# Two-layer graph attention with top-p sparsification: trial sums of the extra tiles on ScalarE, residuals of the output rows by an identity product

## The chip, the cores and the metric

The kernel runs on one core of a Trainium2 chip. The metric is device time in microseconds (us) of one execution; a lower figure is better. Engines are named as the profile names them: PE (TensorE), DVE (VectorE), ACT (ScalarE), POOL (GpSimd) and SP (SyncE, which here only issues transfers). Each runs its own instructions in order and waits for others by semaphores.

## The reference

There are N = 3327 nodes with D = 256 features, in float32. Layer 0 is a graph attention over a sparse adjacency matrix, followed by a gated recurrent unit, a residual and a layer normalisation. Layer 1 takes its result X (called x1 below) and makes two steps over all nodes:

```
R  = (S + I) / row sums                  # S: the sparse adjacency
for n in 0, 1:
    A  = top_p_attention(Xa)             # softmax of q k^T, then the largest entries of
                                         # each row until their sum reaches 0.9
    Xf = R @ Xf ;  Xa = A @ Xa
    Z  = Z + Xf @ U1[n].T + Xa @ U2[n].T
h   = X + Z
out = layernorm(x1 + (layernorm(h) * ln_g + ln_b))
```

A row's nucleus is found without a full sort: a kept entry is one above a threshold of that row, and the sum of the entries above a trial value tells on which side of the threshold the trial lies.

## The kernel before, in words

Rows are worked on in 26 tiles of 128 (the last has 127). A "product" i is one tile of one step, 0 to 25 in step 0 and 26 to 51 in step 1.

Layer 0 comes first (`Layer0.run`). Towards its end, `first_logits` (L1010) computes the logits of the first two tiles of step 0, group by group as the keys come in, on a list of column chunks (`FIRST_CHUNKS`).

Layer 1 (`Layer1`, from L1120) loads U1, U2, ln_g and ln_b at its start. Then `run` (L1752) loops over the products. Product i multiplies the kept probabilities of tile i with the features (`turn` and `times`: PE transposes, ACT copies `at`, PE products `pav`, in seven groups). Between the groups there are seven slots, and `slot(g, f)` puts other work behind group g: the logits of tile i + 2, the exponentials and the list of the largest entries of tile i + 1, the residue of tile i - 1 (`rest`). `propagate` (L1355) is the sparse product with R: POOL gathers the neighbours' rows (L607) and makes one-hot weights `m` (L1353), PE multiplies (`pxf`, L1361), ACT scales, POOL adds the own row (L1366, L1367), SP stores the result to DRAM.

Rows whose nucleus the fast method does not settle are flagged (`flag`, counted by a small product `pos`, L1486), put aside in a list in DRAM (`left_over`, L1516), and computed again as three "extra" tiles h0, h1 and h2 (`HARD` = 3) with a more thorough method. For an extra tile k:

- `hard_load` (L1521) reads the list from DRAM and gathers the rows (four gathers, one of them later in `hard_gather`).
- `hard_q`, `hard_exp` (L1543, L1562) compute its logits (PE) and their exponentials (ACT), 3327 wide.
- `bound` (L1575) narrows the threshold from above: for each of six factors f in `CUTS` (1/16, 1/4, 1/2, 0.71, 0.84, 0.92) it sums the entries below f times the present bound by one wide DVE pass (`kept_sum`, L1336) and multiplies the bound by f where the sum is large enough. Each trial depends on the one before.
- `hard` (L1592) is the search itself on DVE: one wide pass (L1598), the largest entries of each group of columns, their sort, a scan, three wide replacements (L1330) and a last wide pass (L1627).
- `hard_end` (L1633) is its product with the features and its output rows, `hard_store` (L1659) the scatter of the rows to the output.

`ends` (L1697) follows product 51. It runs the searches of h0, h1 and h2 and, between their steps, the output of the 26 tiles. A tile's output (`tile_end`, L1454) is a generator of some eight stages: loads of xf, xf2 and xa2; transposes and their copies (`ptxut`, `ptxvt`, L1176, L1178); the products with U1 and U2 into `pzt` (L1430); and `output_rows` (L1435). That copies the sum to SBUF (L1438), adds x1 on POOL (L1439), takes mean and variance on DVE (`moments`: L1374, L1376, and two POOL operations at L1377, L1378), normalises on ACT (`normalized`: a shift of 128x1 by POOL at L1384, then L1385), multiplies by ln_g, adds ln_b and adds x1 on POOL (L1445, L1446, L1447), and normalises once more. `tick` opens one tile and moves every open one a stage on. `more` moves the first job of a queue (the start of h2, the ends of h0 and h1) one step, and calls `tick` in every call when the queue was empty and in every second call otherwise. `ends` calls `more` after each step of a trial or a search. Last comes `hard_end` of h2 with its output rows.

In Layer 1 the order on PE, ACT and DVE is that of the program text. The order on POOL and SP is made by a scheduler when the kernel is built.

Of the kernel before, what the change touches and what calls it, by code (L numbers as in the profile page):

```python
# [53 lines left out]
FIRST_CHUNKS = [[(h, s, LC) for h in range(2)] for s in range(0, HALF - LC, LC)] + [  # L54
    [(0, HALF - LC, LC), (1, HALF - LC, LATE - HALF + LC)]
]
# [12 lines left out]

CUTS = tuple(2.0 ** -f for f in (4.0, 2.0, 1.0, 0.5, 0.25, 0.125))  # L70
# [446 lines left out]
class Shared:  # L517


    def __init__(self, tc, ctx, x, W1T, W2T, W3T):  # L520
# [48 lines left out]

        self.xa_rows = dram.tile([N, D], F32, name="xa_rows")  # L570
# [70 lines left out]
class Layer0:  # L641
# [364 lines left out]
    def first_logits(self):  # L1006


        nc, sh = self.nc, self.sh
        while not self.searched:  # L1010
            yield
        for chunks in FIRST_CHUNKS:
            while self.done * P < chunks[-1][0] * HALF + chunks[-1][1] + chunks[-1][2]:
                yield
            for i in range(2):
                on = [slice(h * DA, (h + 1) * DA) for h, _, _ in chunks]
                pls = [
                    self.ps.tile([P, 512], F32, tag="tr", name=f"first{i}_{h}_{s}") for h, s, _ in chunks
                ]
                for pl, half, (h, s, w) in zip(pls, on, chunks):  # L1020
                    nc.tensor.matmul(
                        pl[:, :w], sh.qT[half, cols(i)], sh.kT[half, 0, s : s + w], start=True, stop=True
                    )
                yield
                for pl, (h, s, w) in zip(pls, chunks):
                    nc.scalar.copy(sh.arrays[i][:, h * HALF + s : h * HALF + s + w], pl[:, :w])
                yield
                if i == 0:
                    for h, s, w in chunks:
                        for g in range(s // GROUP[0], (s + w) // GROUP[0]):  # L1030
                            c = h * HALF + g * GROUP[0]
                            at = c // GROUP[0] * 8
                            nc.vector.max(sh.cand[:, at : at + 8], sh.arrays[0][:, c : c + GROUP[0]])
                    yield
# [86 lines left out]
class Layer1:  # L1121
    def __init__(self, sh, ctx, U1T, U2T, ln_g, ln_b, out):
# [12 lines left out]
        nc.scalar.dma_start(self.u1, U1T.rearrange("s (c p) d -> p (s c) d", p=P))  # L1135
        self.u2 = keep.tile([P, STEPS * DC, D], F32, name="u2")
        nc.scalar.dma_start(self.u2, U2T.rearrange("s (c p) d -> p (s c) d", p=P))
        self.g = keep.tile([P, D], F32, name="ln_g")
        nc.scalar.dma_start(self.g, ln_g.partition_broadcast(P))
        self.b = keep.tile([P, D], F32, name="ln_b")  # L1140
        nc.scalar.dma_start(self.b, ln_b.partition_broadcast(P))
# [8 lines left out]
        self.p = [sh.arrays[2][:, :N], keep.tile([P, N], F32, name="p")]  # L1150

# [203 lines left out]
    def propagate(self, i):  # L1355
# [12 lines left out]
        move_rows(nc.sync, (sh.xf2_rows if v.n else sh.xf_rows)[t * P : t * P + r, :], v.xf2, r)  # L1368

# [11 lines left out]
    def normalized(self, dst, src, mv, r, tag):  # L1381
        nc = self.nc
        shift = self.small("shift", f"shift{tag}")
        nc.gpsimd.tensor_scalar(shift[:r], mv[:r, 0:1], mv[:r, 1:2], -1.0, ALU.mult, ALU.mult)  # L1384
        nc.scalar.activation(dst, src, AF.Identity, bias=shift[:r], scale=mv[:r, 1:2])  # L1385
# [49 lines left out]
    def output_rows(self, pz, x1, h, r, tag):  # L1435
# [3 lines left out]
        nc.gpsimd.tensor_tensor(h, h, x1, ALU.add)  # L1439
        yield  # L1440
# [5 lines left out]
        nc.gpsimd.tensor_tensor(h, h, self.b[:r], ALU.add)  # L1446
        nc.gpsimd.tensor_tensor(h, h, x1, ALU.add)  # L1447
# [6 lines left out]
    def tile_end(self, t):  # L1454
# [4 lines left out]
        xa2 = self.work.tile([P, D], F32, tag="xf", name=f"xa2_{t}")  # L1459
        move_rows(nc.sync, a[:r, :D], sh.xf_rows[on, :], r)  # L1460
        move_rows(nc.sync, a[:r, D : 2 * D], sh.xf2_rows[on, :], r)
        move_rows(nc.sync, xa2[:r], sh.xa2_rows[on, :], r)
        yield
# [6 lines left out]
        for n, xt in enumerate(xts):  # L1470
            self.output_terms(pz, xt, n, (0, 1), r, n == 0, n == 1)
        yield

        k = t % (N // D)
        h = sh.qT[:r, k * D : (k + 1) * D]
        yield from self.output_rows(pz, sh.x1[:r, t, :], h, r, f"t{t}")
        move_rows(nc.sync, self.out[on, :], h, r)
# [65 lines left out]
    def hard_q(self, k):  # L1543
# [8 lines left out]
        if k == 1:  # L1552
            a, b = self.p
        else:
            a, b = (self.l[j % 2][:, :N] for j in (k // 2, k // 2 + 1))
        v.p, v.other = a, b

        v.top = self.small("htop", f"top{v.tag}")
# [16 lines left out]
    def bound(self, k):  # L1575
# [3 lines left out]
        v.thr = self.small("hthr", f"thr{tag}")  # L1579
        nc.gpsimd.tensor_scalar(v.thr, v.pay[:, 2:3], 0.5, None, ALU.mult)  # L1580
        for i, f in enumerate(CUTS):
# [5 lines left out]
            nxt = self.small("top", f"top{tag}_{i + 1}")  # L1587
# [45 lines left out]
    def hard_end(self, k):  # L1633
# [20 lines left out]
        self.output_terms(pz, xt, 1, (1,), P, False, True)  # L1654
        v.o = xa
        v.end = self.output_rows(pz, x1, v.o, P, v.tag)
# [40 lines left out]
    def ends(self, bound):  # L1697
# [11 lines left out]
        def more():  # L1709
            self.calls += 1  # L1710
            busy = bool(queue)
            if busy and next(queue[0], True):
                queue.pop(0)
            if not busy or self.calls % 2:
                tick()

        self.calls = 0

        def start(k):
            self.hard_q(k)  # L1720
            for pair in self.chunks():
                yield
                self.hard_exp(k, pair)

# [4 lines left out]
        for _ in start(1):  # L1729
            pass  # L1730
        for _ in bound:
            more()
        for k in range(HARD):
            for j, _ in enumerate(self.hard(k)):
                if k == 0 and j == 2:
# [191 lines left out]
```

## Time and profile before

| | |
|---|---|
| median of the runs | 1890.84 us (1890.25 to 1891.82, 3 runs) |
| the profiled execution | 1894.84 us |
| its span | 1893.1 us |
| mean granted clock of PE | 0.941 |

| stage | from, to (us) | length |
|---|---|---|
| layer 0 | 0 to 432 | 432 |
| step 0 of layer 1 | 432 to about 1010 | 578 |
| step 1 | about 1020 to 1597 | 577 |
| trial sums of h0 | 1597 to 1624 | 27 |
| searches of h0, h1, h2 with the output of the tiles | 1624 to 1847 | 223 |
| product and output of h2 | 1847 to 1893 | 46 |

A span is what the profiler saw from the first to the last instruction; a busy time is the sum of an engine's instructions in a stretch, without issuing of transfers and without waits. In a row of groups the figures behind the bar are busy time, mean duration of one instruction in ns, and the idle time just before them with what ended it. A PE duration is that of one instruction, and several overlap: eight products of 128x256 follow each other in 1.73 us.

### The profile page before, as it was taken

What the parts mean: (1) busy time and instruction counts of PE and PEld (TensorE: products, weight loads), DVE (VectorE), ACT (ScalarE), POOL (GpSimd) and SP (SyncE); (2) the same over time, 40 slices, a digit from 0 to 9 for tenths busy, and PEclk for the clock granted to TensorE, in tenths of its full rate; (3) what the DMA queues carried; (4) which work ended last, traced back from release to release, by engine and by line L of the source; (5) the groups of instructions that cost most, each with busy time, mean ns of one, the idle gap of its engine ahead of it and who ended that gap; (6) DMA issues with size and microseconds to landing.
All of it is one profiled execution on the core that took longest, in us unless ns stands there. A gap on an engine that the chain in (4) does not pass through costs nothing.

```text
span 1893.1 us, 27173 instructions
## 1 busy us (share of the span) xinstructions
PE 1662.6 (88%) x8035; PEld 1218.2 (64%) x8035; DVE 1371.5 (72%) x4318; ACT 918.7 (49%) x2063; POOL 1222.8 (65%) x1900
## 2 busy tenths in 40 slices
PE   6578778987999999999996999999999998988844
PEld 4345545555777777777774777777777676676733
DVE  6789886436556665556654999999999897978771
ACT  3245445544565555565553555555555453434332
POOL 1477778837766666666654566556666574699993
PEclk9789889997999999999997999999999998999977
DMA  9766652212211111111101111111111121212100
GB/s 328 261 213 233 200 172 68 63 35 79 59 40 40 40 42 48 48 40 40 39 29 50 48 49 45 45 48 56 51 48 45 46 59 31 60 59 79 56 28 20
DMA packets 84205, 143.96 MB, mean 76 GB/s; under 512 B 15561, under 2 KB 57283, under 8 KB 84050
## 3 DMA queue, kind: packets, MB, share of 16 engines
q1 hardware_dynamic: 52288, 78.38, 12.4%
q0 software_dynamic: 20384, 53.28, 10.7%
q10 hardware_dynamic: 11378, 10.49, 1.7%
q8 instruction: 66, 1.08, 0.2%
q14 instruction: 89, 0.73, 0.1%
HBM read 117.84 MB, written 24.35 MB: 75 GB/s over the span
## 4 chain that ended last, share of the span: by engine, by line
PE 38%; DVE 33%; POOL 12%; ACT 6%; DMA 6%; issue 4%; ACTq 0%; POOLq 0%; DVEq 0%; SPq 0%
PE pav L1410 18%; DVE array L1330 6%; PE pl L1192 5%; DVE cand L1208 4%; PE pxf L1361 4%; PE pt L1394 4%; DVE cand L1228 3%; DMA g<-whx,edge 3%; POOL g L607 3%; DVE lst L1226 3%; DVE p L1316 2%; DVE array L1316 2%; DVE at L812 2%; ACT at L1396 1%; DMA array<-in_adj_dram 1%
## 5 line engine op out<-in xcount | busy, mean ns | idle before, releaser
L1410 PE MATMUL pav<-xa,at 128*128 128x256 f32 (+2 forms) x1352 | 330.0, 389 | 7.0 <-ACT at L1396 7.0
L1410 PE MATMUL pav<-x,at 128*128 128x256 f32 (+2 forms) x1352 | 326.8, 386 | 7.3 <-ACT at L1396 7.3
L1396 ACT COPY at<-pt 128x512 f32<-128x512 f32 (+2 forms) x364 | 191.9, 541 | 269.3 <-PE pt L1394 268.2
L1410 PEld LDWEIGHTS pav<-xa,at 128*128 128x128 f32 (+2 forms) x1352 | 245.5, 191 | 85.1 <-ACT at L1396 38.9
L1410 PEld LDWEIGHTS pav<-x,at 128*128 128x128 f32 (+2 forms) x1352 | 245.4, 191 | 72.1 <-ACT at L1396 29.7
L1208 DVE MAX8 cand<-array 128x8 f32<-128x167 f32 (+5 forms) x921 | 238.8, 336 | 46.9 <-ACT array L1195 46.9
L1195 ACT COPY array<-pl 128x416 f32<-128x416 f32 (+4 forms) x405 | 182.9, 502 | 183.6 <-PE pl L1192 183.5
L607 POOL DMA_INDIRECT g<-xf_rows,edge x130 | 135.7, 1044 | 164.9 <-PE pxf L1361 132.6
L607 POOL DMA_INDIRECT g<-x_rows,edge x130 | 133.7, 1029 | 128.2 <-PE ptq L620 91.4
L1192 PE MATMUL pl<-kT,qT 64*128 64x416 f32 (+4 forms) x810 | 197.6, 561 | 1.8 <-ACT kT L637 1.8
L1300 DVE TENSOR_TENSOR_SCAN before<-e 128x40 f32<-128x40 f32 (+3 forms) x52 | 14.3, 274 | 216.4 <-ACT e L1293 216.4
L607 POOL DMA_INDIRECT g<-whx,edge x130 | 136.9, 1053 | 46.6 <-issue 31.1
L1353 POOL TENSOR_SCALAR m<-col,erow 128x128 f32<-128x128 f32 x260 | 159.6, 628 | 10.0 <-PE pxf L1361 8.0
L1361 PE MATMUL pxf<-g,m 128*128 128x256 f32 (+1 forms) x520 | 134.5, 408 | 11.2 <-DVE out L1238 5.9
L1361 PEld LDWEIGHTS pxf<-g,m 128*128 128x128 f32 (+1 forms) x520 | 99.4, 200 | 65.7 <-issue 39.6
L1226 DVE MAX8 lst<-cand 128x8 f32<-128x160 f32 (+3 forms) x364 | 114.5, 315 | 9.0
L1394 PE MATMUL pt<-ident,array 128*128 128x128 f32 (+1 forms) x676 | 101.5, 277 | 6.2 <-DVE array L1316 6.2
L812 DVE FIND_INDEX8 at<-ones,array 128x8 uint32<-128x840 f32 (+1 forms) x104 | 106.5, 1026 | 0.0
L1394 PE MATMUL pt<-ident,p 128*128 128x128 f32 (+2 forms) x676 | 100.4, 275 | 4.5 <-DVE p L1316 4.5
L1394 PEld LDWEIGHTS pt<-ident,array 128*128 128x128 f32 (+1 forms) x676 | 85.2, 145 | 24.7 <-PE pxf L1361 8.2
L1394 PEld LDWEIGHTS pt<-ident,p 128*128 128x128 f32 (+2 forms) x676 | 84.6, 144 | 22.0 <-PE pxf L1361 8.6
L965 PE MATMUL prz<-wih,hT 128*128 128x512 f32 (+1 forms) x104 | 68.1, 790 | 34.3 <-ACT hT L963 34.3
(373 smaller groups left out, 3366.0 us busy)
## 6 DMA issues: line engine op xcount, KB each, us to landing
array<-in_adj_dram SPq DMA_DIRECT2D x25, 1248.0 KB
array<-in_adj_dram SPq DMA_DIRECT2D x25, 415.5 KB
xf_rows<-xf SPq DMA_DIRECT2D x50, 128.0 KB
xa_rows<-xa SPq DMA_DIRECT2D x50, 128.0 KB
xfs<-xf_rows SPq DMA_DIRECT2D x50, 128.0 KB
whx<-table ACTq DMA_DIRECT2D x25, 129.5 KB
x_rows<-x ACTq DMA_DIRECT2D x25, 128.0 KB
xf<-xf_rows SPq DMA_DIRECT2D x25, 128.0 KB
```

What stands on the lines that cost most here:

```text
L607: self.nc.gpsimd.indirect_dma_start(out=dst[:, b, :], out_offset=None, in_=table[:, :], in_offset=bass.IndirectOffsetOnAxis(ap=self.edge[: ...
L812: nc.vector.max_index(at[:r, g, :], self.ones8[:r], ad[:r, g, :])
L1192: nc.tensor.matmul(pl[:r, :w], q[on], self.sh.kT[on, n, s : s + w], start=True, stop=True)
L1195: nc.scalar.copy(l[:r, h * HALF + s : h * HALF + s + w], pl[:r, :w])
L1208: self.nc.vector.max(cand[:r, g * 8 : g * 8 + 8], src[:r, g * group : min(N, (g + 1) * group)])
L1226: nc.vector.max(lst[:r, k : k + 8], cand[:r])
L1330: nc.vector.match_replace(rev, gone[:r], rev, -BIG)
L1353: nc.gpsimd.tensor_scalar(v.m[:, b, :], sh.col1, sh.erow[:, v.at, b : b + 1], None, ALU.is_equal)
L1361: nc.tensor.matmul(acc[:r, :D], v.m[:, b, :r], v.g[:, b, :], start=(b == 0), stop=(b == EB - 1))
L1394: nc.tensor.transpose(pt[: rows(j), j - j0, :r], v.p[:r, cols(j)], self.ident[:r, :r])
L1396: nc.scalar.copy(at[:, :full, :r], pt[:, :full, :r])
L1410: nc.tensor.matmul(v.acc[: v.r, :D], at[:k, j - 4 * g, : v.r], V[:k, j, :], start=(j == 0), stop=(j == NT - 1))
```

## The change

1. `FIRST_CHUNKS` is ordered anew: one group of the first half's last columns comes first, and the last group has two chunks of 288 columns in place of two of 416 and two of 288.
2. U1, U2, ln_g and ln_b are loaded by SP's queue instead of ACT's.
3. `propagate` of step 0 also computes xb = x1 + ln_b for each tile (one POOL addition) and stores it in DRAM. `tile_end` loads x1 and xb for its tile, into columns of a buffer that is free by then.
4. In the output rows the first residual is added by a product with the identity matrix into the same accumulation (`plus`), not by POOL. After ln_g, one POOL addition of xb takes the place of two, of ln_b and x1. Extra tiles keep both. The shift is two ACT copies of 128x1 with a scale, no longer a POOL operation.
5. The first trials of an extra tile are computed by ACT (`coarse_bound`): per trial and half of the columns one Relu and one Sign with accumulation, from which nine small POOL operations make the sum and the new bound. h0 has two such trials, in products 50 and 51, and four on DVE; h1 and h2 have three and three.
6. `hard_load` of h0 and h1 moves from slot 5 to slot 0 of product 48; `hard_q` of h0 from product 50 to 48, its exponentials to 49, those of h1 to 50. The probabilities of h0 and h1 lie in what was x1's buffer.
7. In `ends` the start of h2 is queued at once, `tick` runs in every call of `more`, each call also takes up to two steps of the coarse trials, `hard_end` of h2 goes through the queue, and all `hard_store` come last.

```diff
-FIRST_CHUNKS = [[(h, s, LC) for h in range(2)] for s in range(0, HALF - LC, LC)] + [
-    [(0, HALF - LC, LC), (1, HALF - LC, LATE - HALF + LC)]
-]
+FIRST_CHUNKS = [[(i, 0, HALF - LC, LC) for i in range(2)]]
+FIRST_CHUNKS += [[(i, h, s, LC) for h in range(2)] for s in range(0, HALF - LC, LC) for i in range(2)]
+FIRST_CHUNKS += [[(i, 1, HALF - LC, LATE - HALF + LC) for i in range(2)]]
...
-        nc.scalar.dma_start(self.u1, U1T.rearrange("s (c p) d -> p (s c) d", p=P))
+        nc.sync.dma_start(self.u1, U1T.rearrange("s (c p) d -> p (s c) d", p=P))
...
+        if v.n == 0:
+            xb = self.work.tile([P, D], F32, tag="xa2", name=f"xb{t}")
+            nc.gpsimd.tensor_tensor(xb[:r], v.xf, self.b[:r], ALU.add)
+            move_rows(nc.sync, sh.xb_rows[t * P : t * P + r, :], xb[:r], r)
...
-        nc.gpsimd.tensor_scalar(shift[:r], mv[:r, 0:1], mv[:r, 1:2], -1.0, ALU.mult, ALU.mult)
+        nc.scalar.activation(shift[:r], mv[:r, 0:1], AF.Copy, scale=-1.0)
+        nc.scalar.activation(shift[:r], shift[:r], AF.Copy, scale=mv[:r, 1:2])
...
-        nc.gpsimd.tensor_tensor(h, h, x1, ALU.add)
...
-        nc.gpsimd.tensor_tensor(h, h, self.b[:r], ALU.add)
-        nc.gpsimd.tensor_tensor(h, h, x1, ALU.add)
+        for term in terms:
+            nc.gpsimd.tensor_tensor(h, h, term, ALU.add)
...
+        move_rows(nc.sync, x1, sh.x1_rows[on, :], r)
...
+        self.plus(pz, x1, r)
...
+        move_rows(nc.sync, xb, sh.xb_rows[on, :], r)
+        yield from self.output_rows(pz, [xb], h, r, f"t{t}")
...
+    def plus(self, pz, x, r):
+        self.nc.tensor.matmul(pz[:r, :D], self.ident[:r, :r], x, start=False, stop=True)
...
+    def coarse_bound(self, k, cuts, junk):
...
+        for f in cuts:
+            nc.gpsimd.tensor_scalar(minus, v.top, -f, None, ALU.mult)
...
+            for h in range(2):
+                on = slice(h * HALF, min(N, (h + 1) * HALF))
+                for j, func in enumerate((AF.Relu, AF.Sign)):
+                    nc.scalar.activation(
+                        junk[:, on], v.p[:, on], func, bias=minus, accum_out=s[:, 2 * h + j : 2 * h + j + 1]
+                    )
+                    if h == 0 or j == 0:
+                        yield
+            nc.gpsimd.tensor_tensor(both, s[:, 0:2], s[:, 2:4], ALU.add)
+            nc.gpsimd.tensor_scalar(number, both[:, 1:2], 0.5, 0.5 * N, ALU.mult, ALU.add)
+            nc.gpsimd.tensor_tensor(number, number, minus, ALU.mult)
+            nc.gpsimd.tensor_tensor(number, both[:, 0:1], number, ALU.subtract)
+            nc.gpsimd.tensor_scalar(up, number, less, f - 1.0, ALU.is_lt, ALU.mult)
+            nc.gpsimd.tensor_scalar(up, up, 1.0, None, ALU.add)
+            nc.gpsimd.tensor_tensor(nxt, up, v.top, ALU.mult)
...
         def more():
-            self.calls += 1
-            busy = bool(queue)
-            if busy and next(queue[0], True):
+            if queue and next(queue[0], True):
                 queue.pop(0)
-            if not busy or self.calls % 2:
-                tick()
+            tick()
+            for _ in range(2):
+                for g in bounds:
+                    if not next(g, True):
+                        break
...
+        queue.append(start(2))
+        for k in range(HARD):
+            if k:
+                for _ in bounds[k - 1]:
+                    pass
+                for _ in self.bound(k, CUTS[COARSE:]):
+                    more()
+            for _ in self.hard(k):
+                more()
+            queue.append(end(k))
...
-                    slot(5, self.hard_load, 0)
-                    slot(5, self.hard_load, 1)
+                    slot(0, self.hard_load, 0)
+                    slot(0, self.hard_load, 1)
+                if i == total - 4:
+                    slot(6, self.hard_q, 0)
                 if i == total - 2:
-                    slot(3, self.hard_q, 0)
-                    for k, pair in enumerate(self.chunks()):
-                        slot(3 + k, self.hard_exp, 0, pair)
+                    slot(3, self.hard_q, 1)
+                for k, at, first in ((0, total - 3, 0), (1, total - 2, 3)):
+                    if i == at:
+                        for j, pair in enumerate(self.chunks()):
+                            slot(first + j, self.hard_exp, k, pair)
+                if total - 2 <= i:
+                    coarse = self.coarse_bound(0, CUTS[i - total + 2 :][:1], self.l[0][:, :N])
+                    for g in (0, 1, 2, 3) if i == total - 2 else (0, 0, 1, 1):
+                        slot(g, next, coarse, None)
...
                 if i + 1 == total:
-                    bound = self.bound(0)
-                    for g in (1, 3, 5):
-                        slot(g, next, bound)
+                    bound = self.bound(0, CUTS[2:])
+                    bounds = [self.coarse_bound(1, CUTS[:COARSE], self.l[1][:, :N])]
+                    for g in (2, 3, 4, 5, 6):
+                        slot(g, next, bound, None)
+                    for g in (3, 4, 5, 6):
+                        slot(g, next, bounds[0], None)
```

## The prediction

> **What bounds the kernel now.** I read the page first (engines, then the costliest groups), then a table of stretches of the last 300 us, the groups of that stretch, the waits, and single stretches in order of time. On the page:
>
> ```profile
> PE 1662.6 (88%) x8035; PEld 1218.2 (64%) x8035; DVE 1371.5 (72%) x4318; ACT 918.7 (49%) x2063; POOL 1222.8 (65%) x1900
> ```
>
> TensorE leads on average, but the change touches several stages with different limits. Step 0 (432 to 1010 us) runs on TensorE and step 1 (1020 to 1597) on TensorE and VectorE together, at 21.8 us a tile in both. After 1597 comes the end stage. Columns of the next view: stretch, length, busy us (instructions) of PE, weight loads, DVE, ACT, POOL, then clock, DMA share, GB/s.
>
> ```profile
> 1020.00:1590.00 570.00, 532.53 (x2626) 397.87 (x2626) 521.47 (x1628) 292.83 (x572) 340.16 (x588) 0.97 0.17 47
> 1597.00:1624.00 27.00, 24.86 (x113) 17.84 (x114) 25.30 (x29) 11.13 (x24) 21.67 (x9) 0.92 0.21 45
> 1624.00:1847.20 223.20, 171.83 (x851) 143.12 (x851) 182.27 (x385) 79.41 (x167) 192.19 (x291) 0.91 0.18 57
> 1847.20:1893.00 45.80, 22.52 (x105) 18.57 (x103) 3.42 (x14) 9.91 (x20) 14.80 (x30) 0.72 0.06 21
> ```
>
> First the trial sums of extra tile h0, then the three searches on DVE, then h2's product alone. In the 223.2 us no engine is full: POOL 192, DVE 182, PE 172. They wait for each other. The groups after 1597 say how:
>
> ```profile
> L1336 DVE SCALAR_TENSOR_TENSOR array<-array,cndh 128x3327 f32<-128x3327 f32 x12 | 45.2, 3765 | 2.2 <-ACT array L1573 1.7
> L1336 DVE SCALAR_TENSOR_TENSOR p<-array,cndh 128x3327 f32<-128x3327 f32 x6 | 22.9, 3818 | 0.3
> L1374 DVE BATCH_NORM_STATS2 bnbt<-qT 128x6 f32<-128x256 f32 (+1 forms) x26 | 10.9, 421 | 23.6 <-POOL qT L1447 23.5
> L1385 ACT ACTIVATE qT<-qT,shiftbt,mvbt 128x256 f32<-128x256 f32 (+1 forms) x26 | 15.7, 604 | 35.4 <-POOL shiftbt L1384 35.4
> L1384 POOL TENSOR_SCALAR shiftbt<-mvbt 128x1 f32<-128x1 f32 (+1 forms) x26 | 22.5, 865 | 0.7
> L1439 POOL TENSOR_TENSOR qT<-qT,x 128x256 f32<-128x256 f32 (+1 forms) x26 | 18.9, 725 | 6.9 <-ACT qT L1438 6.9
> ```
>
> The 18 trial sums are DVE work; DVE waits 23.5 us for POOL's last residual add, and ACT 35.4 us for POOL's shift, a 128x1 operation of 865 ns. Single instructions tell why it is so long:
>
> ```profile
> 1654.46 3.69 DVE L1627 SCALAR_TENSOR_TENSOR array<-array,th 128x3327 f32<-128x3327 f32 x1
> 1654.55 4.18 POOL L1447 TENSOR_TENSOR qT<-qT,x 128x256 f32<-128x256 f32 x1
> ```
>
> The same add takes 0.73 at 1850: a POOL operation that starts under a wide DVE pass lasts until the pass ends. And in step 1, product 49:
>
> ```profile
> 1569.02 0.16 PE L1486 MATMUL pos<-flag,lower 128*128 128x1 bf16 x1 [8.15 <-POOL flag L1484]
> ```
>
> POOL is late there with the gathers of the extra tiles (1539 to 1551); that product takes 32.5 us instead of 21.8.
>
> **What the Trainium skill says.** "SBUF — State Buffer", Who interferes with whom: a VectorE operation with two SBUF inputs blocks a GpSimd operation that reads SBUF, fully; the 4.18 us above agrees. "ScalarE: Activation LUTs", What ACT_TABLE_LOAD costs: an activation takes about 280 ns + 0.833 ns an element with a pointer operand, 186 + 0.833 with immediates. For 1664 columns that is an estimate of 1.67 us; the trace has 1.684 plus 0.191 for reading the accumulator (L1280). The same section prices a switch of function set at 2.66 us; the built order has no more switches after the change than before, so I add none.
>
> **The change part by part.** Against the profiled execution: 1894.84 us, which is 1893.1 of span and 1.74 outside it; it lies 4.0 us above the median of the runs.
>
> (1) Boundary of the layers. The four weight loads leave ACT's queue (issues from 423.9 to 428.4; the copy after them starts at 428.48) and the last group of first logits has two products of 288 columns instead of four products. The SP queue takes the loads and has room. -3 us (-4 to 0).
>
> (2) xb = x1 + ln_b in step 0: 26 POOL adds of 0.73 (L1439's row) and 26 stores of 128 KB. Two buffers, so an add waits for the store of the one two before; a 128 KB store lands in 1.7 to 1.84 (issue at 457.74, the waiting load at 459.44). Two adds per 2.65 us. In the built order POOL has twenty of them in one block between the own rows of tile 1 (469.3) and the gathers of tile 3, which ran at 490 to 497 and are wanted by TensorE at 509.4. Twenty take 27 us, with one or two caught under a DVE pass 34. The block ends at 497 to 504, the five gathers (6.7) and the m (2.9) at 507 to 514. +3 us (0 to +20), and TensorE at 98.8% in step 0 can't win it back.
>
> (3) Products 48 to 50. hard_load comes five slots earlier: its gathers and the wait for the list leave the place that cost the 8.15, and the clock that dropped behind it (some 2.5). It now stands ahead of the flag in product 48 (+5.5, estimated from two landings of 2.2 and 2.9). hard_q and hard_exp of h0 and h1 move into full products: 16 records at 0.97 for four, 3.9 us of TensorE each, against as much less later; h0's counts here (+3.5), h1's is taken with part 5. Four half-row passes on ACT in product 50 are 7.1, half of it before the list's exponentials: +3.6. Sum +2 (-6 to +8).
>
> (4) h0's trial sums. Before, six passes of 4.36 ran from 1597.9 and the search began at 1624.0. After, two cuts are ACT's. Cut 1/4 needs four passes (1.78 each with overlap) between the at copies of the last product, so about 1600 to 1611, then seven POOL operations (2.2), behind the residual, the index work and six gathers: about 1617. Then four passes, 17.4. Search at 1635 rather than 1624: +11 (+3 to +20). Here the change loses: ACT plus POOL is slower than two DVE passes.
>
> (5) Searches. Of DVE's 182.3 in the long stretch, 6 of 12 passes go: 26.2. The coarse sums of h1 and h2 are 24 ACT passes, 43 us against 144 us of idle ACT. POOL loses L1439 (18.9), both L1384 rows (29.3) and one of L1446/L1447 (25 to 29), and gets some 45 small operations of 0.2 to 0.29. Net some 63 of 192 gone, and fewer long passes to be caught under. Cost: two 128x1 copies instead of each shift, 0.19 and 0.28 by the page's formula (nearest row: 0.297 for L1559), 58 pairs, 27 us of ACT. TensorE: the identity product, 8 records of an equal shape take 1.73, so two take 0.43, 29 of them 13 us. The added loads, 52 of 128 KB at 6 to 9% DMA share, are hidden by the call before.
> DVE needs 156; at 90% it is 173, from 1637 to 1810. TensorE needs 24.9 + 171.8 + 13 - 4 (h1's logits) = 206 from 1599, at the 94% that it held from 1597 to 1700 (96.5 of 103) 219: 1818. They are coupled by the order of the calls, so I take 1820 for the end of h2's search, against 1847.2: -27, of which parts 3 and 4 have already taken 13 back.
>
> (6) The last 45.8. ACT waits 7.0 and 3.7 us for POOL's shifts here, at 1848 and 1853, in front of h2's copies. Both go, as does L1439 in h2's rows (0.73); one identity product and two more row stores come: 39.5 (37 to 44), -6.3.
>
> Sum: -3 + 3 - 27.2 - 6.3 = -33.7; 1861.1 as a profiled run, 1857 on the scale of the median.
>
> **The rivals.**
> A, the ends run better: DVE at 97% in part 5 gives 1798 for h2's search, TensorE following; 1835. For it: POOL was the only engine to hold DVE. Against: TensorE's own 206.
> B, TensorE becomes the bound. tick() at every call puts a tile's 5.7 us beside a quarter of an extra product's 28, 12 us of TensorE in calls where DVE has 5.6. With 85% of TensorE, 206 becomes 242, the search ends at 1841 and the kernel at 1878. For it: 52 us of TensorE idle before; against: much of that was POOL's.
> C, the other side: ACT, in program order, holds TensorE. A trial pass stands between the transposes and the copy that feeds the output product; the 24 passes are 43 us. If all are exposed, 1857 + 43 = 1900. It decides from 34 us on, four passes in five. For it: more() sends up to two steps of trial passes at every call, right behind tick(). Against: DVE needs 5 us a call anyway and ACT 5 to 7.
> D, part 2 costs more: each add waits for its own store behind SP's other transfers, 3.7 us instead of 1.35, block +47 us less 8 of slack: 1857 + 36 = 1893. For it: one POOL queue, twenty in a row; against: the 1.7 us measured.
> That nothing happens: not likely, since six passes and 63 us of POOL leave the stretch that sets the end.
>
> **How the numbers follow.** Forecast (1845 to 1868) 0.50, A 0.12, B 0.20, C 0.11, D 0.07. Runs spread by 0.1% and the profile by 0.2%, so 0.2% (3.8 us) is what a measurement can tell. C ends slower in most of its chance and D in half: slower 0.14, same 0.04, faster 0.82. The range 1834 to 1890 leaves out the fast half of A, and C; with the ends of parts 2 and 4 inside it.
>
> **What would show it.** Ten trial passes (L1336) instead of 18, six of them after h0's; DVE's wait for POOL's last add below 8 us; no shift on POOL. h0's search starts at 1630 to 1640, h2's ends near 1820. In step 0, the product of tile 3 late by 0 to 5 us once. No wait over 4 us on the flag in product 49, a new one in 48. Wrong would be: TensorE idle for ACT's copies for more than 30 us after 1600 (C), POOL's block over 40 us (D), or h0's search later than 1645, with DVE idle for the coarse cut.

## The result and the profile after

The changed kernel takes 1886.91 us (median of 14 runs, 1884.41 to 1889.88), the kernel before 1894.18 us in the 14 runs taken with them. The ratio is 0.9963, with a 95% interval of 0.9953 to 0.9974: about 7 us faster. The forecast was 34 us faster, at 1857. The time lies in the range given, but only a fifth of the gain is there. The profiled execution has a span of 1884.5 us against 1893.1.

The page of the kernel after, busy time by engine:

```profile
PE 1665.2 (88%) x8093; PEld 1223.3 (65%) x8093; DVE 1335.0 (71%) x4278; ACT 997.8 (53%) x2243; POOL 1174.2 (62%) x1881
```

DVE lost 36.5 us and POOL 49, ACT gained 79: the work moved as the change says. The same stretches as in the prediction, with the columns given there: step 1, then from the start of product 51 to h0's search, then the three searches, and last h2's product alone.

```profile
1020.00:1590.00 570.00, 530.21 (x2623) 394.62 (x2623) 519.37 (x1623) 296.81 (x578) 335.81 (x582) 0.97 0.18 49
1608.80:1645.50 36.70, 22.21 (x109) 17.64 (x109) 16.88 (x20) 24.74 (x39) 21.21 (x29) 0.87 0.22 51
1645.50:1844.20 198.70, 173.71 (x889) 147.12 (x888) 151.04 (x348) 129.09 (x297) 126.09 (x216) 0.96 0.30 91
1844.20:1884.50 40.30, 21.35 (x107) 17.82 (x107) 4.73 (x20) 13.61 (x36) 13.82 (x25) 0.80 0.07 24
```

The searches hold 31 us less of DVE's work and 66 less of POOL's, and are 24.5 us shorter. Still no engine is full. The groups of the end stage name the new wait:

```profile
L1337 DVE SCALAR_TENSOR_TENSOR array<-x,cndh 128x3327 f32<-128x3327 f32 x7 | 27.0, 3860 | 0.3
L1337 DVE SCALAR_TENSOR_TENSOR p<-array,cndh 128x3327 f32<-128x3327 f32 x3 | 11.9, 3961 | 0.2
L1379 DVE BATCH_NORM_STATS2 bnbt<-qT 128x6 f32<-128x256 f32 (+1 forms) x26 | 10.9, 419 | 12.2 <-POOL qT L1451 12.1
L1379 DVE BATCH_NORM_STATS2 bnat<-qT 128x6 f32<-128x256 f32 (+1 forms) x26 | 10.6, 406 | 27.1 <-ACT qT L1444 27.1
```

Ten trial passes are left of 18. DVE's wait for POOL's last addition has halved (most of what is left, 8.8, comes after h2's search). In its place DVE waits 27.1 us for the copy of a tile's sum (L1444), which before cost it nothing, and 12.3 us for the same copy of an extra tile's rows. That is 39.4 of the 47.7 us in which DVE stands idle during the searches: it now waits for what TensorE and ACT make.

One edit that the list of the change does not name bears on this. Before, `output_rows` had two `yield`s between a tile's sum and its statistics; now it has one:

```diff
         nc.scalar.copy(h, pz[:r, :D])
-        nc.gpsimd.tensor_tensor(h, h, x1, ALU.add)
-        yield
         yield
         m = self.moments(h, r, f"a{tag}")
```

So DVE asks for a sum one call of `more` earlier than before. No run put the second `yield` back, and how much of the 27.1 us is due to it stays open.

Start by start, this is where the time went. "Later" is measured against the kernel before, in the profiled executions.

| point | before | after | later by | step of the prediction | its forecast | measured |
|---|---|---|---|---|---|---|
| product 1 of step 0 | 465.69 | 463.17 | -2.5 | 1, boundary | -3 | -2.5 |
| product 4 | 531.21 | 533.07 | +1.9 | 2, xb | +3 | +4.4 |
| product 47 | 1494.48 | 1494.83 | +0.4 | change of step, not forecast | 0 | -1.5 |
| product 51 | 1596.85 | 1608.78 | +11.9 | 3, products 48 to 50 | +2 | +11.5 |
| h0's search | 1624.04 | 1645.51 | +21.5 | 4, h0's trials | +11 | +9.5 |
| h2's search ends | 1847.2 | 1844.2 | -3.0 | 5, searches | -40.2 | -24.5 |
| end | 1893.1 | 1884.5 | -8.6 | 6, h2's product | -6.3 | -5.6 |

A product starts with its first `pxf`. (The prediction wrote part 5 as -27.2, with the 13 of parts 3 and 4 in it.) Two steps failed, part 3 by 9.5 us and part 5 by 15.7. The others are within 1.5.

The first three rows are small against the spread of single profiles. Over the sixteen profiled kernels that have xb, product 1 starts at 460.3 to 466.2, product 4 comes 65.7 to 70.1 us after it (65.5 before), and product 47 comes 961.4 to 965.5 us after product 4 (963.3 before). So -2.5, +4.4 and -1.5 are what this one pair shows, not prices.

What is seen in the two places? In product 47, PE in order of time has a wait that the kernel before did not have there, and POOL's queue (some lines left out) says why:

```profile
1523.43 0.16 PE L1497 MATMUL pos<-flag,lower 128*128 128x1 bf16 x1 [6.74 <-POOL flag L1495]
```

```profile
1514.11 0.18 POOL L1539 CAST idxh<-payh 128x1 uint32<-128x1 f32 x1 [2.89 <-DMA payh<-left_over]
1516.41 1.15 POOL L1548 DMA_INDIRECT xh<-xa_rows,idxh  x1 [0.16 <-POOL pay L1511]
1517.64 2.51 POOL L1253 TENSOR_SCALAR many<-d 128x1 f32<-128x1 f32 x1
1520.43 1.11 POOL L1548 DMA_INDIRECT xh<-x_rows,idxh  x1 [0.28 <-issue]
1521.59 0.31 POOL L1254 TENSOR_SCALAR flag<-many,short 128x1 f32<-128x1 f32 x1
```

The load of h0 stands ahead of the flag of the tile. POOL waits for the list to land, gathers, and computes the flag in between. TensorE waits for it.

In product 51, DVE stands until ACT and POOL have done the cut 1/4 of h0 (the form is "who waits for whom: us in all, times, longest"):

```profile
DVE cndh L1625 <- POOL toph_0.25_16379 L1613: 20.0, 1, 20.0
```

In the end stage, ACT in order of time stands for a trial value, TensorE stands for ACT, and POOL, which owes the value, is under DVE's passes:

```profile
1640.77 1.68 ACT L1598 ACTIVATE array<-x,minush_0.25_16522 128x1664 f32<-128x1664 f32 x1 [7.70 <-POOL minush_0.25_16522 L1593]
```

```profile
1644.90 2.25 PE L1578 MATMUL plh<-kT,qh 64*128 64x416 f32 x4 [8.56 <-ACT array L1581]
1692.71 3.78 PE L1416 MATMUL pavh<-xa,ath 128*128 128x256 f32 x8 [9.89 <-ACT ath L1402]
```

```profile
1632.92 3.56 POOL L1610 TENSOR_SCALAR up4h_0.0625_16492<-many4h_0.0625_16488,lessh 128x1 f32<-128x1 f32 x1
1636.56 0.22 POOL L1611 TENSOR_SCALAR up4h_0.0625_16492<-up4h_0.0625_16492 128x1 f32<-128x1 f32 x1
1636.86 0.19 POOL L1613 TENSOR_TENSOR toph_0.0625_16495<-up4h_0.0625_16492,toph 128x1 f32<-128x1 f32 x1
1637.14 3.60 POOL L1593 TENSOR_SCALAR minush_0.25_16522<-toph_0.0625_16495 128x1 f32<-128x1 f32 x1
```

Two of these operations on 128 numbers take 3.6 us, the length of a pass of h0 on DVE; the two between take 0.2. (A trial has eight such operations, and the first trial of a tile one more.) So the trial chain of h1 on ACT and POOL runs into h0's trials on DVE, and what is queued behind it on ACT (h2's exponentials, the tiles' copies, `ath`) waits too. TensorE has 35.5 and 38.3 us busy in the two stretches of 50 us from 1600 to 1700, then 48.0 and 48.9 in the next two. (Before, it had 45.5 and 48.0, then 37.6 and 40.4.)

### The profile page after: what moved, and what is told of

It is laid out like the page before. It is cut to its first block, busy times and chain, and to the rows that moved or that the text cites. A ratio compares the mean times of both kernels' runs of the same rounds, so it can differ in the third digit from the quotient of the medians.

```text
span 1884.5 us, 27520 instructions
## 1 busy us (share of the span) xinstructions
PE 1665.2 (88%) x8093; PEld 1223.3 (65%) x8093; DVE 1335.0 (71%) x4278; ACT 997.8 (53%) x2243; POOL 1174.2 (62%) x1881
## 5 line engine op out<-in xcount | busy, mean ns | idle before, releaser
L609 POOL DMA_INDIRECT g<-x_rows,edge x130 | 140.3, 1079 | 104.4 <-PE ptq L622 71.3
```

The lines of the kernel that those rows point to most:

```text
L609: self.nc.gpsimd.indirect_dma_start(out=dst[:, b, :], out_offset=None, in_=table[:, :], in_offset=bass.IndirectOffsetOnAxis(ap=self.edge[: ...
```

## The experiments

Each changes the kernel after; the lines that matter are shown, and "..." marks what is left out. Ratios are to the kernel before; 0.001 is 1.9 us. The change itself has 0.9963 (0.9953 to 0.9974), and gains and losses against it are differences of ratios. With both intervals, such a difference is good to 3 to 5 us. Readings of a stretch come from one profile of each kernel. Theory T says that ACT, in program order, holds the others at the start of the end stage. B is the prediction's rival that TensorE's own work sets the end. L says that the calls of `more` put too much of TensorE ahead of DVE's next step.

**All six trials of h0 on DVE.**

```diff
-                    coarse = self.coarse_bound(0, CUTS[i - total + 2 :][:1], self.l[0][:, :N])
-                    for g in (0, 1, 2, 3) if i == total - 2 else (0, 0, 1, 1):
-                        slot(g, next, coarse, None)
...
-                    bound = self.bound(0, CUTS[2:])
+                    bound = self.bound(0, CUTS)
```

> The changed kernel with all six trial sums of h0 on DVE and none on ACT; h0's logits and exponentials stay in products 48 and 49. Theory T (ACT, in program order, holds TensorE and DVE at the start of the end stage; TensorE makes up for it later at full load): h0's search starts at 1634 to 1637 in place of 1645.5 (six passes of 4.36 from 1608), ACT has eight passes (14 us) less before 1623, and the end comes 8 to 11 us earlier than with the change: about 1877. Rival B (TensorE's own work from 1611 on sets the end): the search starts as early, but the end moves by 3 us at most.

Measured 1883.22 us, 0.9939 (0.9916 to 0.9962), some 4.5 us better than the change (the two intervals just overlap), half of what T said. Product 51 starts at 1602.9, so that h0's passes on ACT had cost product 50 5.6 of the 11.5 us (it takes 23.7 instead of 29.3). The search starts at 1629, 16.5 us earlier. But it ends at 1673.5 and takes 44.5 us, not 34.6. The waits of this run say why:

```profile
PE plh L1578 <- ACT array L1581: 13.5, 1, 13.5
ACT array L1598 <- POOL minush_0.25_16498 L1593: 12.7, 1, 12.7
```

With more passes on DVE, what stands in POOL's queue, h1's chain and the gathers ahead of it (shown below), is blocked longer, and that takes back what h0 won.

**One step of ACT's trials per call instead of two.**

```diff
-            for _ in range(2):
+            for _ in range(1):
```

> The changed kernel with one step of the trial sums on ACT per call instead of two. Theory T: TensorE's waits for ACT between 1600 and 1700 (9.9 for ath, 8.6 for the exponentials) get shorter and the end comes 3 to 8 us earlier. Rival B: no difference over 2 us. Should the last steps of h1 now stand in a row before its search, DVE shows a wait of 5 us or more there and the end comes later.

1888.18 us, 0.9975 (0.9966 to 0.9984): no gain. DVE's waits for the tiles' sums fall from 27.1 to 11.3 us, but DVE now waits 5.6 and 10.5 us for the last trial ahead of h1 and h2, as the last sentence of the expectation had it. This slower pace moves the wait and does not shorten it.

**No trials on ACT for h1 and h2.**

```diff
-COARSE = 3
+COARSE = 0
```

> The changed kernel with all six trial sums of h1 and of h2 on DVE (h0 keeps its two on ACT). DVE gets six passes of 4.36, 26.2 us, more; ACT loses 24 passes, 43 us. Theory T: what DVE pays comes back from ACT, since TensorE no longer waits 19 us for it before 1700: the end within 5 us of the change's. If DVE set the pace, 18 to 26 us later; if TensorE's own work did, earlier by no more than 3.

1903.46 us, 1.0049 (1.0031 to 1.0066), 16 us worse than the change. T's number was wrong: DVE's 26.2 us come back to 16, not to nothing. At the end TensorE now waits for DVE (`PE pth <- DVE array`, 38.3 us in one wait). So the trial passes on ACT are worth their place. If all of DVE's 26.2 us are exposed here, what the passes on ACT cost is the rest, some 10 us; the run that leaves them out, below, measures it.

**Step 1 as before.**

```diff
-                    slot(0, self.hard_load, 0)
-                    slot(0, self.hard_load, 1)
+                    slot(5, self.hard_load, 0)
+                    slot(5, self.hard_load, 1)
...
-                    slot(3, self.hard_q, 1)
+                    slot(3, self.hard_q, 0)
...
+        for _ in start(1):
+            pass
```

> The changed kernel with step 1 as before: loads of h0 and h1 back in slot 5 of product 48, h0's logits and exponentials back in product 50, h1's in the end stage, all six trials of h0 on DVE; h1 and h2 keep three on ACT. Product 51 should start at about 1597 instead of 1608.8. Theory T: h0's search starts at 1625, and the end comes 12 to 20 us earlier than with the change, 1867 to 1875. Rival B: TensorE gets h1's 4 us back in the end stage, so 7 us earlier, 1880.

1894.12 us, 1.0003 (0.9992 to 1.0014): 7.6 us worse than the change, where T and B both said better. Product 51 starts at 1595.8 and h0's search at 1623.0, 22 us earlier, and all of it is lost. h1's logits, exponentials and trials come after 1600, and the end stage has more to do: DVE's waits for the tiles' sums grow from 27 to 56.5 us.

```profile
DVE bnat L1379 <- ACT qT L1444: 56.5, 13, 15.6
```

**The old rule for opening tiles.**

```diff
-            tick()
+            if not busy or self.calls % 2:
+                tick()
```

> The changed kernel with the old rule for the output tiles: in calls in which the queue has work, a new tile is opened and the open ones move on only in every second call. Lockstep theory L (a tile's 6 us of TensorE beside a quarter of an extra product in one call make DVE wait for the tile's sum, 27 us in all, since the tile's statistics stand ahead of the next search step on DVE): DVE's waits for the sums fall under 12 us, h2's search ends 8 to 15 us before the 1844 of the change; some four tiles are then left for the last 40 us, and take back up to 10. The end 0 to 10 us earlier. If the waits come from ACT's trial passes alone: no change in the waits, and the end 5 to 10 later for the tiles left over.

1893.35 us, 0.9994 (0.9983 to 1.0006), 6 us worse. L was right on the search and wrong on the rest. DVE's waits for the sums are 5.1 us up to the end of h2's search, and that search ends at 1818, 26 us before the change's. But TensorE has 42 us of work left then, against 21 with the change, and a tile's stages pass from engine to engine: the kernel ends 72 us after the search, not 40.

**The first residual of the tiles on POOL.**

```diff
-        h, x1, xb = spare(t % 6), spare(6 + t % 3), spare(9 + t % 3)
+        h, x1, xb = spare(t % 5), spare(5 + t % 4), spare(9 + t % 3)
...
-        self.plus(pz, x1, r)
...
+            nc.gpsimd.tensor_tensor(h, h, x1, ALU.add)
```

> The changed kernel with the first residual of the 26 tiles added by POOL again (0.73 each) and not by the identity product; extra tiles keep the product. TensorE has 13 us less, POOL 19 us more. Rival B (TensorE's own work sets the end): 8 to 12 us earlier. If the coupling of the engines sets it: from 3 earlier to 6 later, since the sum reaches DVE one POOL operation later.

1897.23 us, 1.0016 (1.0004 to 1.0027), 10 us worse with 11 us less of TensorE. DVE now waits for that addition, which lies under its own passes:

```profile
DVE bnat L1379 <- POOL qT L1446: 41.2, 13, 10.5
ACT qT L1444 <- DMA out_dram<-qT: 27.7, 20, 3.7
```

The second line is not the addition's. In this run x1 is needed one stage longer, so the rows of a tile have five buffers in place of six, and ACT's copies wait 27.7 us for the stores that free them; with the change that wait is nothing. How the 10 us divide between the addition and these waits was not separated.

**The shift on POOL.**

```diff
-        nc.scalar.activation(shift[:r], mv[:r, 0:1], AF.Copy, scale=-1.0)
-        nc.scalar.activation(shift[:r], shift[:r], AF.Copy, scale=mv[:r, 1:2])
+        nc.gpsimd.tensor_scalar(shift[:r], mv[:r, 0:1], mv[:r, 1:2], -1.0, ALU.mult, ALU.mult)
```

> The changed kernel with the shift computed by one POOL operation again in place of two ACT copies. ACT has some 27 us less, POOL gets 58 operations of 0.26 bare, more under DVE's wide passes. If ACT's order holds the end stage (theory T): 3 to 8 us earlier. If POOL's blocked operations cost what the prediction gave them: 5 to 12 us later.

1891.21 us, 0.9993 (0.9978 to 1.0008): about 5.7 us worse, with wide limits. Two copies on ACT take 0.19 to 0.22 and 0.29 us, close to the 0.19 and 0.28 that the prediction estimated from the Trainium skill's "ScalarE: Activation LUTs", What ACT_TABLE_LOAD costs. They pay.

**Without xb.**

```diff
-            xb = self.work.tile([P, D], F32, tag="xa2", name=f"xb{t}")
-            nc.gpsimd.tensor_tensor(xb[:r], v.xf, self.b[:r], ALU.add)
...
+        yield from self.output_rows(pz, [self.b[:r], x1], h, r, f"t{t}")
```

> The changed kernel without xb: no addition and store in step 0, no load of it in the end stage; ln_b and x1 are added by two POOL operations as before. Product 4 should start at 529 instead of 533, 3 to 5 us that hold to the end of step 1 in part (the change of step takes some). In the end stage POOL gets 26 additions, 19 to 25 us. Sum: from 4 us earlier to 4 later; if POOL is no bound there any more, earlier.

1888.92 us, 0.9983 (0.9974 to 0.9991), 3.8 us worse. Product 4 starts 65.5 us after product 1, not 69.9 as with the change. That alone does not price xb: two of the runs below that keep it (trials left out, finer steps) have 65.7. The end stage, from the start of h0's search, is 4.9 us longer in the profile; DVE's wait for POOL's last addition grows from 12.1 to 22.2 us.

**The first residual left out.**

```diff
-        self.plus(pz, x1, r)
```

> The changed kernel with the first residual of the 26 tiles left out (no identity product and no addition; extra tiles keep theirs): TensorE has 26 products of 0.43, 11 us, less and nobody gets them. It prices TensorE's work by itself, which the run with POOL's addition could not. Rival B (TensorE's own work sets the end): 8 to 11 us earlier than with the change. Theory T: TensorE is full only from 1700 to 1800, where half of the products lie: 3 to 7 us earlier.

1886.01 us, 0.9956 (0.9941 to 0.9972): 1.3 us better than the change, within the limits of both, with 11 us of TensorE gone. TensorE's amount of work does not set the end: B said at least 8 us. T's 3 to 7 us did not come either, or only its lower end.

**Trials of h1 and h2 left out on ACT.**

```diff
-            bounds.append(self.coarse_bound(k, CUTS[:COARSE], self.items[f"h{k}"].other))
+            bounds.append(iter(()))
```

> The changed kernel with the first three trials of h1 and h2 left out altogether (their searches start from a looser bound; three trials each stay on DVE): ACT has 24 passes, 43 us, and POOL the small operations less, the rest is the same. It prices what the trials on ACT still cost. Theory T (ACT in program order, and the chain of small POOL operations behind DVE's passes, keep TensorE short of work before 1700, and that is missed later): the end 10 to 20 us earlier than with the change. If ACT's idle time hides the passes, as the prediction had it: within 3 us.

With the loose bound the run went on into the general method and took 10.5 ms, so only the fast part of the profile is read. The searches:

```profile
1648.80:1836.00 187.20, 158.32 (x825) 135.89 (x823) 150.33 (x348) 93.21 (x250) 117.75 (x177) 0.95 0.31 93
```

DVE has the same 150 us as with the change, in 187.2 us instead of 198.7. The 24 passes, which the prediction set against ACT's idle time, cost 11.5 us, with the small POOL operations that belong to them. They reach DVE by its waits for the sums: for tiles and extra tiles together these are 28.6 us here, not 39.4.

**The same passes without their chain.**

```diff
-            nc.gpsimd.tensor_scalar(minus, v.top, -f, None, ALU.mult)
+            nc.gpsimd.tensor_scalar(minus, v.pay[:, 2:3], -f, None, ALU.mult)
```

> The changed kernel with the trial values of ACT's passes taken from a number that each row has from the start, not from the result of the trial before: all passes and all small POOL operations are there, but a pass waits for no earlier one. The bounds that come out are not the right ones, so that the run may go on into the general method after the fast part; only the end stage of the profile is read. Chain theory: ACT's waits for POOL (7.7 and 3.5 us before 1700) are gone, and h2's search takes 5 to 9 us less from the start of h0's (198.6 with the change, 187.2 without the passes). If the passes' length counts: within 3 us of 198.6.

```profile
1649.20:1843.50 194.30, 167.52 (x859) 142.61 (x860) 150.81 (x348) 123.56 (x289) 128.07 (x212) 0.96 0.31 93
```

4.4 us less than with the change, a little under what the chain theory gave (this is one execution). DVE's waits for the sums are 35.2 us, 4.2 less. Of the 11.5, then, 4.4 are the waiting for the trial before, and 7 belong to the passes in ACT's order and the small operations in POOL's; these two were not separated.

**Finer steps of the extra products.**

```diff
-            if g % 2:
-                yield
+            yield
```

> The changed kernel with the product of an extra tile cut into seven steps of one group instead of four steps of two, so that a call holds 3.7 us of it beside a tile's 6 us, not 7. Lockstep theory L: DVE's waits for the sums (27 us) and for the extra tiles' rows (12 us) fall by a third and h2's search ends 5 to 10 us earlier; the end too. If TensorE's total work sets the end: within 2 us.

1882.56 us, 0.9937 (0.9920 to 0.9954), 5 us better. The searches take 193.7 us instead of 198.7; DVE waits 21 us for the sums instead of 27, and 11 for the extra tiles' rows instead of 12. L holds in direction and in the time gained; the waits fell by less than the third that it said.

**h1's logits in product 51.**

```diff
-                for k, at, first in ((0, total - 3, 0), (1, total - 2, 3)):
+                if total - 2 <= i:
+                    k = i - total + 2
+                    first = 0 if k else 3
...
```

> The changed kernel with all six trials of h0 on DVE, the loads of h0 and h1 back in slot 5 of product 48, h0's logits and exponentials back in product 50, and h1's in product 51, where DVE has nothing but h0's trials. Product 51 should start at 1597 and h0's search at 1625; h1's trials on ACT follow in the end stage. If step 1's 12 us are a true loss: the end 6 to 12 us earlier than with the change, below the run with h0's trials on DVE alone (ratio 0.9939). If what step 1 wins is lost again in the end stage, as in the run with step 1 as before: no earlier than that run.

1893.62 us, 0.9987 (0.9979 to 0.9995). Again step 1 wins 12.8 us (product 51 at 1596.0), h0's search starts at 1623.3, and the end is 4.5 us later than with the change: TensorE waits 15.8 us for ACT, which stands 12.2 us of them for POOL at h1's first trial value, and DVE's waits for the sums are 50.3 us. A shorter step 1 is worth nothing while these waits take it.

**Both edits that helped**, h0's trials on DVE and the finer steps, in one kernel. The next run adds its diff to this one, and the last run adds its own to both.

> The changed kernel with all six trials of h0 on DVE and the extra products in steps of one group: the two edits that gave 4.5 and 5 us alone. If they free different places (ACT before 1630; DVE's waits after 1700): ratio 0.991 to 0.992 against 0.9963 of the change. If both only move the same wait: 0.9935 to 0.994 as each alone.

1878.94 us, 0.9916 (0.9895 to 0.9937). They add up, within the limits. The wait of ACT is still there, and POOL in order of time (lines left out before the last) shows the length of it: six gathers, 1.0 us each when alone, are ahead of the chain, and the first four run under h0's passes. They are h2's and the late ones of h0 and h1.

```profile
1620.72 3.94 POOL L1548 DMA_INDIRECT xh<-x_rows,idxh  x1 [0.30 <-issue]
1624.96 4.04 POOL L1548 DMA_INDIRECT xh<-xf_rows,idxh  x1 [0.30 <-issue]
1629.31 3.86 POOL L1548 DMA_INDIRECT xh<-xf_rows,idxh  x1 [0.30 <-issue]
1633.47 1.00 POOL L1548 DMA_INDIRECT xh<-xf_rows,idxh  x1 [0.30 <-issue]
1637.91 0.22 POOL L1593 TENSOR_SCALAR minush_0.25_16498<-toph_0.0625_16471 128x1 f32<-128x1 f32 x1
```

```profile
1638.16 1.68 ACT L1598 ACTIVATE array<-x,minush_0.25_16498 128x1664 f32<-128x1664 f32 x1 [13.43 <-POOL minush_0.25_16498 L1593]
```

**And h1's trials only after product 51.**

```diff
-                    for g in (3, 4, 5, 6):
-                        slot(g, next, bounds[0], None)
```

> As c1_h0_dve_fine, and the trials of h1 on ACT begin only in the end stage, not in product 51 beside h0's six passes on DVE. In the run with h0's trials on DVE, ACT stood 12.7 us for the trial value of h1's second cut, which POOL could not finish under DVE's passes, and TensorE stood 13.5 us behind ACT. Chain theory: both waits fall under 4 us and the end comes 3 to 8 us earlier than in c1_h0_dve_fine. If the length of ACT's passes counts: no change over 2 us, since they are only moved.

1866.89 us, 0.9856 (0.9839 to 0.9874), 12 us better, more than the 3 to 8 expected. The same instruction of ACT waits 2.92 us, and TensorE's wait of 14.2 us for the exponentials is down to 1.9:

```profile
1639.99 1.68 ACT L1598 ACTIVATE array<-x,minush_0.25_16594 128x1664 f32<-128x1664 f32 x1 [2.92 <-POOL minush_0.25_16594 L1593]
```

No pass was taken out, they begin ten us later. POOL gives the trial value no earlier than before; but ACT meanwhile does what stood behind the passes. All of TensorE's waits for ACT after 1596 are 21.5 us instead of 34.1, about as much less as the end gained. h0's search takes 34.6 us again, and TensorE is busy for 43.3 of the 50 us after 1600 instead of 31.6.

**And the loads of h0 and h1 behind the flags.**

```diff
-                    slot(0, self.hard_load, 0)
-                    slot(0, self.hard_load, 1)
-                if i == total - 4:
-                    slot(6, self.hard_q, 0)
+                    slot(3, self.hard_load, 0)
+                    slot(6, self.hard_load, 1)
...
+                if i == total - 3:
+                    slot(3, self.hard_q, 0)
```

> As c2_late_trials, with the loads of h0 and h1 in slots 3 and 6 of product 48, so that POOL's queue has them behind the flags of tiles 22 and 23, and h0's logits and exponentials in slots 3 on of product 49. If the loads ahead of the flag are what product 48 lost: TensorE's wait of 6.7 us for the flag at 1523 is gone, product 49 starts 5 to 7 us earlier, and at least half of that is left at the start of product 51. If the loss only moves on to product 49 or 50, as with the kernel before: product 51 starts within 2 us of c2_late_trials.

1858.87 us, 0.9816 (0.9799 to 0.9832). The wait for the flag in product 47 is gone, product 48 starts at 1518.4 and product 51 at 1596.0, 7.7 us earlier than in the run before this, and all of it reaches the end. This version is faster than both kernels: its searches and its last stretch are

```profile
1622.10:1817.50 195.40, 171.30 (x889) 147.06 (x890) 149.37 (x346) 133.91 (x301) 129.65 (x224) 0.97 0.32 97
1817.50:1856.90 39.40, 23.05 (x107) 19.11 (x107) 5.38 (x22) 15.41 (x42) 16.82 (x31) 0.76 0.08 28
```

## Why the prediction was right and wrong

**Part 1** (boundary, -3) and **part 6** (-6.3, h2's product 39.5) came out as said: -2.5 and -5.6, with 40.3. For part 1 the spread of product 1 over the runs (6 us) is larger than the gain, so that the agreement may be luck.

**Part 2** agrees in this pair of profiles: product 4 late by 4.4 us once, nothing of rival D's 47. But with the same additions and stores the delay was 0.2 to 4.6 us in the other profiles, so +3 is within what was seen and no more is shown.

**Part 3** failed, +11.5 instead of +2. Of its terms, the place of the loads was right (+6.6 for 5.5, in product 47). The term that failed is the gain set against it, the 8.15 and the clock's 2.5: the wait at product 49 went, but from start to start that product still takes 30.9 us, as before (the prediction read 32.5). TensorE's wait was replaced there by h0's 3.9 us of logits, 2.7 us of waits for its exponentials on ACT, and a stretch of eight products that took 3.56 us instead of 1.99. And the passes of h0 in product 50 were 5.6 us, not 3.6, as the run with h0's trials on DVE showed. The last run shows that the loads' place was a true loss: 7.7 us.

**Part 4** was right: from the start of product 51 to h0's search 36.7 us against 27.2, +9.5 for +11, by the passes on ACT, POOL's six gathers and the small operations, as counted. The search began at 1645.5, later than the 1645 that the prediction named as a sign of being wrong, and DVE stood 20.0 us for the coarse cut; but the lateness beyond part 4 is part 3's. What the prediction left open is what that loss is worth. h0's trials back on DVE gave 4.5 us, not 16.5, because another wait took the rest.

**Part 5** is where the gain went: 198.7 us, not 183. The step that failed is "43 us against 144 us of idle ACT", with 10% of waits for DVE. DVE was busy for 151 us, where 156 were said, but idle for 47.7 instead of 17, and 39.4 of these are waits for sums that ACT copies. Idle time of an engine in program order is not a place for passes: the trials stand in front of the tiles' copies and depend on a chain of POOL operations, of which DVE's two-input passes can stretch one to 3.6 us. Leaving the passes out gave 11.5 us of the 15.7, of which 4.4 are the chain. Finer steps of the extra products gave 4.9. (No run made both edits, so that they add up to the 15.7 is not shown.) The prediction counted on "fewer long passes to be caught under" for the work that left POOL, and did not ask the same of the operations that came to it, though it quoted the 4.18 us of L1447. The Trainium skill's page "SBUF — State Buffer", Who interferes with whom, has the rule that a VectorE instruction with two SBUF inputs contends with a GpSimd instruction that reads SBUF, and these traces agree with it: 0.2 us become 3.6.

**The rivals.** B has two halves. That TensorE's amount of work is the bound is refuted (11 us less of TensorE: 1 us). But its mechanism, a tile's work beside a quarter of an extra product in one call, is theory L, and the finer steps gave 4.9 us for it; its figures, TensorE at 85% and h2's search ending at 1841, are near what was measured (83% from product 51 on, and 1844). The prediction gave B 0.20, since it put TensorE's idle time before down to POOL. C named ACT in program order, with a price four times too high: 11.5 us of its 43. The prediction set C against the forecast as all or nothing; a quarter of it was enough to take a third of the gain. Its sign, TensorE idle for ACT for more than 30 us, could not tell: all such waits after 1596 are 37.1 us, and were 42.7 in the kernel before. A did not happen, nor D.

**Open.** How the 7 us divide between the passes' own length on ACT and their small operations on POOL. What the dropped `yield` costs. What the first residual on POOL would cost with six buffers. Why starting h1's trials later gave 12 us, where the run without their chain priced it at 4.4, is explained by the longer wait in that version (13.4 for 7.7) only in part.

## What to carry to other kernels

Work moved to an idle engine has two prices: its length in that engine's program order, and the chain that it waits for. Look at who is queued behind the moved instruction and on which engine each link of its chain runs; here a 0.2 us operation on POOL cost 3.6 us while DVE ran a wide two-input pass. Where two trial chains of different tiles overlap, starting one later can be faster: here ten us later gave 12 us.

## What the runs showed of the hardware

A gather issued by POOL took 1.0 us alone and 3.9 to 4.3 us when it fell under DVE's pass with two SBUF inputs (3.7 us), as POOL's arithmetic does. It is not the length of DVE's pass that does it, as the prediction's "a wide DVE pass" would have it. In the searches of the changed kernel, sixteen POOL additions of 128x256 began under DVE's wide replacements, which take 3.6 us too but have one wide input, and took 0.73 us, as without any pass; the four that began under two-input passes took 4.0 to 4.2 us.

The identity product cost TensorE 0.43 us a tile, and taking it away moved the end by 1 us, within the limits.
